# Splitting the operands of the third down-projection tile one round earlier, into two free weight slots

## The chip, the core and the metric

The kernel runs on one core of a Trainium2 chip. The metric is the device time of one execution in microseconds. A core has a matrix engine (PE, with its weight loads as PEld), a vector engine (DVE), an activation engine (ACT), a general engine (POOL), and SP, which here only issues DMAs. Each takes its instructions from a queue of its own, in order, and waits at the head of the queue until the semaphores that the instruction names have been raised.

## What is computed

The input x is 2 sequences of 1024 rows of 512 numbers. Four sublayers follow one another, each on a layer norm of its input and with a residual: a gated linear attention, a feed-forward block, a softmax attention, and the same feed-forward block again. The change is in the feed-forward block:

```python
def _L0_ffn_ref(x, wq_gate, s_gate, wq_up, s_up, wq_down, s_down):
    def _qlinear(x, wq, scale):
        W = (wq.astype(jnp.float32) - ZERO_POINT) * scale[:, None]
        return jnp.einsum('bsd,hd->bsh', x, W)
    gate = jax.nn.silu(_qlinear(x, wq_gate, s_gate))
    up = _qlinear(x, wq_up, s_up)
    return _qlinear(gate * up, wq_down, s_down)
...
x = x + _L0_attn_a_ref(_layernorm(x), ...)
x = x + _L0_ffn_ref(_layernorm(x), ...)
x = x + _L0_attn_b_ref(_layernorm(x), ...)
x = x + _L0_ffn_ref(_layernorm(x), ...)
```

The hidden width is 1408 = 11 x 128.

## The kernel before

**Halves.** The function `ffn` runs twice: with the name "f" (from x1 to x2) and "g" (from x3 to the output). The 2048 rows are 16 tiles of 128; each `ffn` takes them in two halves `pr` of 8 tiles, so there are four half-blocks: f pr 0, f pr 1, g pr 0 and g pr 1. In each, gate rounds come first and down projections after.

**Gate rounds.** Round `j` (of 11) computes 128 hidden columns for the 8 tiles with seven products P1 to P7 into four PSUM tiles X, Y, Z and V (`products`, L303). Between the products ACT copies X and Z (L728, L731) and DVE combines Y, Z and V (L729 and L732 to L734). `finish` of a round is issued one round later: it adds P2, P3 and P4, ACT applies silu (L702, L703), DVE multiplies gate by up (L705, L706, L709), and the result lies in three places: tiles 0 and 1 in `sg`, tiles 2 and 3 in `ha`, tiles 4 to 7 in `hb`. `finish` of round 10 stands after the loop.

**Splits.** PE multiplies rounded fp32 numbers, so an operand is given as a rounded high part and a remainder. `split` (L85, L86) does that: ACT casts to the high part, DVE (or POOL) subtracts it from the source. The down projection of tile `i` reads its operands, 11 x 128 columns high and as many low, from the tile `hs[i]`. The pool for `hs` has two buffers. Tiles 0 and 1 take them and are split round by round inside `finish`. Tile 2 can be split only when tile 0's last product has read its buffer, tile 3 when tile 1's has, and so on.

**Down projections.** For tile `i`, PE makes 22 products of 128x512: high and low part of each of 11 hidden blocks, by the weights `wd` (L760, L761). DVE scales the sum by `sd_b` (L762), POOL adds the residual `xr` that SP has loaded (L764, L753), and SP stores the tile (L768). Ahead of tile `i` the code splits tile `i`+1, in two pieces of 768 and 640 columns (6 and 5 blocks).

**Other work beside them.** While the tiles run, `late` steps are taken two at a time: in pr 0 those of `combine` for the second half (sums of layer-normed rows on DVE, L244, and splits of 1024 columns into operands named B11, T1, B22, T2, T3, B21 and T4). After f pr 0 the layer norms for the softmax attention (tiles named b0 to b7 here) can begin as soon as their rows of x2 are stored: SP loads `xin_b` (L106), DVE makes statistics (L108 to L112), POOL a power (L114), DVE the normed rows (L116) and a transpose (L187). `behind(done)` puts the `late` steps behind the latest split on the ACT and DVE queues.

**Slots.** A pool of 12 buffers of 128x2048 ("slots") holds gate weights (`wc`, up to three rounds ahead, loaded by L292), the operands made by `combine`, the transposed rows `xT`, and the weights of the attention (`wm`, `wvo`).

**What sets the order.** The program order gives priorities. When the kernel is built, a scheduler with its own idea of durations lays the instructions of every engine into a fixed queue, filling what it takes for gaps with instructions of lower priority, and gives out buffers as they come free in its plan. At run time nothing is reordered.

The loop ahead of the products, before the change:

```python
done = finish(*begun)
wcs = []
for i in range(2 * ST):
    if 1 <= i < 2 * ST - 1:
        n = i + 1
        for js in (slice(0, 6), slice(6, KH)):
            done = h_split(n, js, ha[:, n - 2, js] if n < ST else hb[:, n - ST, js], None)
```

Of the kernel before, what the change touches and what calls it, by code (L numbers as in the profile page):

```python
# [10 lines left out]
F32R = mybir.dt.float32r  # L11
# [5 lines left out]
P = 128  # L17
# [7 lines left out]
KH = HID // P  # L25
ST = 4
# [8 lines left out]
def hybrid_block_kernel(ctx: ExitStack, tc: tile.TileContext, a, out):  # L35
    nc = tc.nc
# [12 lines left out]
    def slot(name, dt=F32R):  # L49

        return wp.tile([P, 2048], dt, tag="slot", name=name)
# [31 lines left out]
    def split(hi, lo, src, eng=None):  # L83

        c = nc.scalar.copy(hi, src)  # L85
        return c.ins, (eng or nc.vector).tensor_tensor(lo, src, hi.bitcast(F32), ALU.subtract).ins  # L86
# [125 lines left out]
    def ln_steps(src, nm, st):  # L212

        return [lambda i=i: ln_norm(src, nm, st, i) for i in range(ST)] + [
            lambda b=b: ln_move(nm, st, b) for b in range(4)
        ]
# [78 lines left out]
    def products(ps, w, nm, pr, n, first):  # L295
        m, x = {
            "P1": (1, "B11"), "P2": (5, "B21"), "P3": (6, "B22"), "P4": (7, "T4"),
            "P5": (2, "T1"), "P6": (3, "T2"), "P7": (4, "T3"),
        }[n]
        o = XT[nm, pr, x]  # L300
        for k in range(2):
            for s in range(2):
                nc.tensor.matmul(  # L303
                    ps,
                    w[:, m, k * P : (k + 1) * P],
                    o[:, s, k, :],
                    start=first and k == 0 and s == 0,
                    stop=k == 1 and s == 1,
                    skip_group_check=n != "P6",
                )  # L310
# [358 lines left out]
    def ffn(src, dst, nm, wcs, after):  # L669


        with ExitStack() as fctx:
            fh = fctx.enter_context(tc.tile_pool(name=f"ffnh{nm}", bufs=1))
            f1 = fctx.enter_context(tc.tile_pool(name=f"ffn1{nm}", bufs=2))
            fw = fctx.enter_context(tc.tile_pool(name=f"ffnw{nm}", bufs=KH))
            fp = fctx.enter_context(tc.tile_pool(name=f"ffn{nm}", bufs=4))
            wd = []
            for pr in range(2):
                if pr == 0:
                    early = ln_steps(src, nm, 2) + ln_steps(src, nm, 3)  # L680
                    late = combine(nm, 1)
                else:
                    early, late = (list(x) for x in after)

                ha = fh.tile([P, 2, KH, P], F32, tag="ha", name=f"ha{nm}{pr}")
                hb = fh.tile([P, ST, KH, P], F32, tag="hb", name=f"hb{nm}{pr}")
                hs = {}

                def h_split(i, js, src, eng):
                    if i not in hs:  # L690
                        hs[i] = f1.tile([P, 2, KH, P], F32R, tag="hs", name=f"hs{nm}{pr}_{i}")
                    return split(hs[i][:, 0, js], hs[i][:, 1, js], src, eng)

                def finish(j, w, X, Z, V, up):

                    products(X, w, nm, pr, "P2", False)
                    products(Z, w, nm, pr, "P3", False)
                    products(V, w, nm, pr, "P4", False)
                    tiles = lambda x: x.rearrange("p (i c) -> p i c", c=P)
                    su = su_s[:, j : j + 1]  # L700
                    sg = fp.tile([P, 512], F32, tag="sg", name=f"sg{nm}{pr}_{j}")
                    nc.scalar.activation(sg, X, AF.Silu, scale=sg_s[:, j : j + 1])  # L702
                    nc.scalar.activation(hb[:, :, j], tiles(Z), AF.Silu, scale=sg_s[:, j : j + 1])  # L703
                    h01 = sg[:, 0:256]
                    nc.vector.scalar_tensor_tensor(h01, V[:, 0:256], su, h01, ALU.mult, ALU.mult)  # L705
                    nc.vector.scalar_tensor_tensor(  # L706
                        ha[:, :, j], tiles(V[:, 256:512]), su, tiles(sg[:, 256:512]), ALU.mult, ALU.mult
                    )
                    nc.vector.scalar_tensor_tensor(hb[:, :, j], tiles(up), su, hb[:, :, j], ALU.mult, ALU.mult)  # L709
                    for i in range(2):  # L710
                        done = h_split(
                            i,
                            j,
                            h01[:, i * P : (i + 1) * P],
                            None if j == KH - 1 or (nm == "f" and pr == 0) else nc.gpsimd,
                        )
                    return done

                begun = None
                for j in range(KH):  # L720
                    for n in range(len(wcs), min(j + 3, KH)):
                        wcs.append(stationary(n, f"{nm}{pr}", (xp, "xres") if nm == "f" and pr == 0 else None))
                    w = wcs[j]
                    X, Y, Z, V = (psum(f"p{n}{nm}{pr}_{j}") for n in "XYZV")
                    for ps, n in ((X, "P1"), (Y, "P6"), (Z, "P5"), (V, "P7")):
                        products(ps, w, nm, pr, n, True)
                    u2 = fp.tile([P, 512], F32, tag="sg", name=f"u2{nm}{pr}_{j}")
                    nc.scalar.copy(u2, X)  # L728
                    nc.vector.tensor_tensor(u2, Y, u2, ALU.add)  # L729
                    up = fp.tile([P, 512], F32, tag="sg", name=f"up{nm}{pr}_{j}")  # L730
                    nc.scalar.copy(up, Z)  # L731
                    nc.vector.tensor_tensor(Z, Z, u2, ALU.add)  # L732
                    nc.vector.tensor_tensor(V, V, u2, ALU.add)
                    nc.vector.tensor_tensor(up, V, up, ALU.add)  # L734
                    if begun:
                        finish(*begun)
                    begun = j, w, X, Z, V, up
                    for _ in range((1, 1, 1, 1, 2, 2, 1, 1, 1, 1, 2)[j] if early else 0):
                        early.pop(0)()
                    if pr == 0:  # L740
                        d = fw.tile([P, 512], F32R, tag="wd", name=f"wd{nm}{j}")
                        nc.sync.dma_start(out=d.bitcast(F32), in_=wd_d[j])
                        wd.append(d)
                done = finish(*begun)
                wcs = []
                for i in range(2 * ST):
                    t = pr * 2 * ST + i
                    if 1 <= i < 2 * ST - 1:
                        n = i + 1
                        for js in (slice(0, 6), slice(6, KH)):  # L750
                            done = h_split(n, js, ha[:, n - 2, js] if n < ST else hb[:, n - ST, js], None)
                    xr = xp.tile([P, D], F32, tag="xres", name=f"xr{nm}{t}")
                    nc.sync.dma_start(out=xr, in_=src[t])  # L753
                    o = fp.tile([P, 512], F32, tag="sg", name=f"o{nm}{t}")

                    last = nm == "g" and t == NT - 1
                    for ds in [slice(0, 256), slice(256, 512)] if last else [slice(0, 512)]:
                        ps = psum(f"po{nm}{t}_{ds.start}")[:, ds]
                        for j in range(KH):
                            nc.tensor.matmul(ps, hs[i][:, 0, j], wd[j][:, ds], start=j == 0, stop=False)  # L760
                            nc.tensor.matmul(ps, hs[i][:, 1, j], wd[j][:, ds], start=False, stop=j == KH - 1)  # L761
                        nc.vector.tensor_tensor(o[:, ds], ps, sd_b[:, ds], ALU.mult)  # L762
                        add = nc.vector if last else nc.gpsimd
                        add.tensor_tensor(xr[:, ds], o[:, ds], xr[:, ds], ALU.add)  # L764
                        if last:
                            nc.sync.dma_start(out=dst[t][:, ds], in_=xr[:, ds])
                    if not last:
                        nc.sync.dma_start(out=dst[t], in_=xr)  # L768
                    with behind(done):
                        for _ in range(2 if i > 0 else 0):  # L770
                            if early or late:
                                (early or late).pop(0)()
                    if pr == 0 and i == 4:
                        wcs = [stationary(n, f"{nm}1") for n in range(2)]

    ffn(
        x1,
        x2,
# [8 lines left out]
    with ExitStack() as bctx:  # L787
# [3 lines left out]
        for dst, d, n in ((wm, m_d, "wm"), (wvo, vo_d, "wvo")):  # L791
            two = [slot(f"{n}{m}") for m in range(2)]
# [228 lines left out]
```

## Time and profile before

| | us |
|---|---|
| three runs | 1000.64, 1002.87, 1003.65 |
| median | 1002.87 |
| the profiled execution | 1001.88 |
| span of its instructions | 1000.2 |
| PE busy in the span | 959.9 (96%) |
| PEld busy | 789.7 (79%) |
| DVE busy | 682.6 (68%) |
| ACT busy | 374.6 (37%) |
| POOL busy | 228.5 (23%) |

The profiled execution is 1.68 us longer than its span, which is what lies around the first and last instruction, and 0.99 us under the median. In the timelines below, times count from the start of the span. The four down-projection stages begin in full at about 341 (f pr 0), 457 (f pr 1), 846 (g pr 0) and 958 us (g pr 1). A line of a timeline has the start, the duration, the engine, the source line and operation, the tiles written and read with the buffer numbers left out, and in brackets the idle time ahead of it with what ended it.

### The profile page before, as it was taken

To read this page: it belongs to the slowest core of one execution; us is meant where nothing else is said; L and a number is where in the kernel's file an instruction comes from. 1 tells how busy PE (TensorE), PEld (TensorE's weight loads), DVE (VectorE), ACT (ScalarE), POOL (GpSimd) and SP (SyncE) were. 2 spreads that over 40 slices of the span, in tenths; PEclk is the share of its full clock that TensorE was granted. 3 is DMA by queue.
4 is the path that set the end of the run, shared out by engine and by line. 5 is a ranking of instruction groups with operands and counts; after the bars stand their busy time and mean duration, and the time that the engine had idled before them with its cause. 6 is when DMAs were issued, how large, how long until landed. Compare 5 with 4: busy or idle time off the path is not lost.

```text
span 1000.2 us, 13108 instructions
## 1 busy us (share of the span) xinstructions
PE 959.9 (96%) x4450; PEld 789.7 (79%) x4450; DVE 682.6 (68%) x1294; ACT 374.6 (37%) x719; POOL 228.5 (23%) x281
## 2 busy tenths in 40 slices
PE   8999999979898999999999999999988999999998
PEld 6788888867686777887888888888866888788877
DVE  6766858769876699786526556356586675976665
ACT  4653334232665433443222223222133443444421
POOL 4442323253644133212200000000000111321122
PEclk9999999989999999999999999999988999999999
DMA  8636463564698555752704766427768763464113
GB/s 265 204 102 169 126 168 129 153 165 157 234 357 234 143 205 203 185 144 74 262 22 94 167 152 163 101 63 153 168 157 288 250 158 66 151 222 163 38 52 96
DMA packets 250996, 160.08 MB, mean 160 GB/s; under 512 B 187760, under 2 KB 203440, under 8 KB 250928
## 3 DMA queue, kind: packets, MB, share of 16 engines
q1 hardware_dynamic: 250928, 159.23, 54.2%
q8 instruction: 35, 0.57, 0.2%
q14 instruction: 33, 0.27, 0.1%
HBM read 102.66 MB, written 41.84 MB: 144 GB/s over the span
## 4 chain that ended last, share of the span: by engine, by line
PE 52%; DMA 3%; DVE 3%; SPq 2%; ACT 1%; issue 0%; POOL 0%; ACTq 0%; POOLq 0%; DVEq 0%
PE pZg L303 4%; PE pVg L303 4%; PE pXg L303 4%; PE pog L761 4%; PE pog L760 4%; PE pob L96 2%; PE psc L96 2%; PE psc L97 2%; PE pob L97 2%; PE pob L98 2%; PE psc L98 2%; PE pYg L303 2%; PE pof L761 2%; PE pVf L303 2%; PE pof L760 2%; PE pZf L303 2%
## 5 line engine op out<-in xcount | busy, mean ns | idle before, releaser
L761 PE MATMUL pof<-wdf,hsf 128*128 128x512 f32 x176 | 68.4, 392 | 4.5 <-DVE hsf L86 4.5
L761 PE MATMUL pog<-wdg,hsg 128*128 128x512 f32 (+1 forms) x187 | 69.0, 378 | 3.0 <-DVE hsg L86 3.0
L760 PE MATMUL pog<-wdg,hsg 128*128 128x512 f32 (+1 forms) x187 | 69.1, 378 | 0.0
L760 PE MATMUL pof<-wdf,hsf 128*128 128x512 f32 x176 | 68.2, 391 | 0.0
L96 PE MATMUL pob<-vh,pth 128*128 128x512 f32 x128 | 51.8, 405 | 5.7 <-ACT pth L85 5.7
L96 PE MATMUL psc<-xh_b,qh 128*128 128x512 f32 x128 | 51.5, 402 | 0.0
L97 PE MATMUL psc<-xT_b,qh 128*128 128x512 f32 x128 | 51.4, 402 | 0.0
L98 PE MATMUL psc<-xh_b,ql 128*128 128x512 f32 x128 | 51.3, 400 | 0.0
L97 PE MATMUL pob<-vl,pth 128*128 128x512 f32 x128 | 51.2, 400 | 0.0
L303 PE MATMUL pXf<-B_f,wcf 128*128 128x512 f32 x176 | 47.8, 401 | 3.4 <-ACT u2f L728 2.3
L98 PE MATMUL pob<-vh,ptl 128*128 128x512 f32 x128 | 50.8, 398 | 0.0
L303 PE MATMUL pVf<-T_f,wcf 128*128 128x512 f32 x176 | 46.7, 392 | 1.4 <-DVE upf L734 0.7
L303 PE MATMUL pXg<-B_g,wcg 128*128 128x512 f32 x176 | 47.2, 389 | 0.0
L303 PE MATMUL pVg<-T_g,wcg 128*128 128x512 f32 x176 | 46.7, 389 | 0.0
L86 POOL TENSOR_TENSOR hsg<-sgg,hsg 128x128 fp32r<-128x128 f32 x40 | 17.6, 461 | 120.9 <-ACT hsg L85 94.9
L837 ACT ACTIVATE pe<-psc,nm 128x512 f32<-128x512 f32 x32 | 21.7, 683 | 62.7 <-DVE nm L832 62.7
L761 PEld LDWEIGHTS pof<-wdf,hsf 128*128 128x128 f32 x176 | 33.1, 188 | 12.7 <-DVE hsf L86 5.9
L761 PEld LDWEIGHTS pog<-wdg,hsg 128*128 128x128 f32 x187 | 35.1, 188 | 10.0 <-DVE hsg L86 3.6
L303 PEld LDWEIGHTS pXf<-B_f,wcf 128*128 128x128 f32 x176 | 33.0, 191 | 12.7 <-ACT u2f L728 3.9
L85 ACT CAST pth<-ptl 128x512 fp32r<-128x512 f32 x30 | 17.1, 618 | 68.0 <-DMA ptl<-p 57.5
L764 POOL TENSOR_TENSOR xrf<-of,xrf 128x512 f32<-128x512 f32 x16 | 25.0, 1563 | 76.6 <-DVE of L762 54.0
L114 POOL TENSOR_TENSOR rs_g<-ve_g,mhalf 128x1 f32<-128x1 f32 x16 | 10.5, 667 | 139.0 <-DVE ve_g L112 123.7
(286 smaller groups left out, 2642.9 us busy)
## 6 DMA issues: line engine op xcount, KB each, us to landing
wcg<-wc SPq DMA_DIRECT2D x22, 896.0 KB, 4.9
wc<-wcf SPq DMA_DIRECT2D x11, 896.0 KB, 4.4
wcf<-wc SPq DMA_DIRECT2D x11, 896.0 KB, 4.9
p<-py SPq DMA_DIRECT2D x15, 512.0 KB, 3.0
ptl<-p SPq DMA_DIRECT2D x60, 128.0 KB, 3.0
xin_a<-in_x SPq DMA_DIRECT2D x16, 256.0 KB, 4.4
xra<-in_x SPq DMA_DIRECT2D x16, 256.0 KB, 3.0
row<-cl SPq DMA_DIRECT2D x16, 256.0 KB, 4.2
```

What stands on the lines that cost most here:

```text
L85: c = nc.scalar.copy(hi, src)
L86: return c.ins, (eng or nc.vector).tensor_tensor(lo, src, hi.bitcast(F32), ALU.subtract).ins
L96: nc.tensor.matmul(ps, lhs_hi, rhs_hi, start=first, stop=False)
L97: nc.tensor.matmul(ps, lhs_hi, rhs_lo, start=False, stop=False)
L98: return nc.tensor.matmul(ps, lhs_lo, rhs_hi, start=False, stop=last).ins
L114: nc.gpsimd.tensor_tensor(rs, ve, mhalf, ALU.pow)
L303: nc.tensor.matmul(ps, w[:, m, k * P : (k + 1) * P], o[:, s, k, :], start=first and k == 0 and s == 0, stop=k == 1 and s == 1, skip_group_ ...
L760: nc.tensor.matmul(ps, hs[i][:, 0, j], wd[j][:, ds], start=j == 0, stop=False)
L761: nc.tensor.matmul(ps, hs[i][:, 1, j], wd[j][:, ds], start=False, stop=j == KH - 1)
L764: add.tensor_tensor(xr[:, ds], o[:, ds], xr[:, ds], ALU.add)
L837: nc.scalar.activation(pe[:, s * 512 : (s + 1) * 512], pS[s], AF.Exp, bias=nm, scale=SC, accum_out=rs[:, s : s + 1],).ins
```

## The change

Tile 2 no longer waits for tile 0's buffer. Its high and low parts get a slot each from the pool of 12. Ten of its eleven hidden blocks are split ahead of the last `finish` (one cast and one subtraction of 1280 columns), the eleventh after it. The loop then splits tile `i`+2 ahead of tile `i`, starting with tile 3 at i = 1. The pool of two `hs` buffers stays and now serves tiles 0, 1, 3, 4, 5, 6 and 7. The numbers of products, evictions, residual adds and transfers stay the same.

```diff
 def h_split(i, js, src, eng):
     if i not in hs:
-        hs[i] = f1.tile([P, 2, KH, P], F32R, tag="hs", name=f"hs{nm}{pr}_{i}")
-    return split(hs[i][:, 0, js], hs[i][:, 1, js], src, eng)
+        if i == 2:
+            two = [slot(f"hs{nm}{pr}_{i}{n}") for n in "hl"]
+            hs[i] = [x[:, 0 : KH * P].rearrange("p (j c) -> p j c", j=KH) for x in two]
+        else:
+            both = f1.tile([P, 2, KH, P], F32R, tag="hs", name=f"hs{nm}{pr}_{i}")
+            hs[i] = both[:, 0], both[:, 1]
+    hi, lo = hs[i]
+    return split(hi[:, js], lo[:, js], src, eng)
...
+h_split(2, slice(0, KH - 1), ha[:, 0, 0 : KH - 1], None)
 done = finish(*begun)
+h_split(2, KH - 1, ha[:, 0, KH - 1], None)
 wcs = []
 for i in range(2 * ST):
     t = pr * 2 * ST + i
-    if 1 <= i < 2 * ST - 1:
-        n = i + 1
+    if 1 <= i < 2 * ST - 2:
+        n = i + 2
         for js in (slice(0, 6), slice(6, KH)):
             done = h_split(n, js, ha[:, n - 2, js] if n < ST else hb[:, n - ST, js], None)
...
-            nc.tensor.matmul(ps, hs[i][:, 0, j], wd[j][:, ds], start=j == 0, stop=False)
-            nc.tensor.matmul(ps, hs[i][:, 1, j], wd[j][:, ds], start=False, stop=j == KH - 1)
+            nc.tensor.matmul(ps, hs[i][0][:, j], wd[j][:, ds], start=j == 0, stop=False)
+            nc.tensor.matmul(ps, hs[i][1][:, j], wd[j][:, ds], start=False, stop=j == KH - 1)
```

## The prediction, made before the changed kernel was run

> **What bounds the kernel now.** I read the page's busy shares first: PE is busy 96% of the span, so a change gains where PE waits, or not at all. The costliest groups come next, for the idle time ahead of the down projections:
>
> ```profile
> L761 PE MATMUL pof<-wdf,hsf 128*128 128x512 f32 x176 | 68.4, 392 | 4.5 <-DVE hsf L86 4.5
> L761 PE MATMUL pog<-wdg,hsg 128*128 128x512 f32 (+1 forms) x187 | 69.0, 378 | 3.0 <-DVE hsg L86 3.0
> ```
>
> The idle time ends with DVE's remainder of `hs`: 7.5 us in all. The PE timeline says where; these are the lines with idle time in the four down-projection stages:
>
> ```profile
> 349.68 0.50 PE L761 MATMUL pof<-wdf,hsf 128*128 128x512 f32 x1 [1.52 <-DVE hsf L86]
> ...
> 366.16 0.50 PE L761 MATMUL pof<-wdf,hsf 128*128 128x512 f32 x1 [1.23 <-DVE hsf L86]
> ...
> 390.60 1.20 PE L303 MATMUL pVf<-T_f,wcf 128*128 128x512 f32 x4 [0.65 <-DVE of L762]
> ...
> 464.71 0.50 PE L761 MATMUL pof<-wdf,hsf 128*128 128x512 f32 x1 [1.48 <-DVE hsf L86]
> ...
> 854.45 0.50 PE L761 MATMUL pog<-wdg,hsg 128*128 128x512 f32 x1 [1.49 <-DVE hsg L86]
> ...
> 966.17 0.50 PE L761 MATMUL pog<-wdg,hsg 128*128 128x512 f32 x1 [1.53 <-DVE hsg L86]
> ```
>
> Four gaps of 1.5 us are the first low part of tile 2, one in each stage. The others, with one of 0.23 at 371.68, lie in f pr 0 and where it runs into f pr 1. The timelines of ACT, DVE and POOL around 462 us show what tile 2 waits for:
>
> ```profile
> 461.84 2.82 ACT L85 CAST hsf<-haf 128x768 fp32r<-128x768 f32 x4 [4.88 <-PE pof L761]
> ...
> 461.79 0.69 DVE L762 TENSOR_TENSOR of<-pof,sd_b 128x512 f32<-128x512 f32 x1 [4.50 <-PE pof L761]
> 462.71 1.94 DVE L86 TENSOR_TENSOR hsf<-haf,hsf 128x768 fp32r<-128x768 f32 x1 [0.23 <-ACT hsf L85]
> ...
> 462.56 1.28 POOL L764 TENSOR_TENSOR xrf<-of,xrf 128x512 f32<-128x512 f32 x1 [9.64 <-DVE of L762]
> ```
>
> Tile 0's last product frees the buffer; then follow tile 0's eviction, the cast, and a subtraction that takes 1.94 us because POOL's add runs beside it (the same shape takes 0.94 at 358.41, with POOL idle). ACT had been idle 4.88 us and DVE 4.50 us just before.
>
> How close DVE is to being the bound: the table by stretches for the end of f pr 0, and DVE's waits from 340 to 400.
>
> ```profile
> 362.00:370.00 8.00, 6.77 (x30) 5.25 (x30) 8.00 (x11) 4.14 (x6) 3.96 (x3) 1.00 0.73 285
> 370.00:378.00 8.00, 7.78 (x35) 6.07 (x34) 8.00 (x10) 4.41 (x5) 3.19 (x2) 1.00 0.41 131
> ...
> DVE bn_b L108 <- DMA xin_b<-x: 2.1, 1, 2.1
> DVE xn_b L116 <- POOL rs_b L114: 1.7, 1, 1.7
> ```
>
> The columns are the stretch, its length, then busy time of PE, PEld, DVE, ACT and POOL. DVE (third) is busy all 8.00 us of both: in this stage DVE sets the pace, PE follows.
>
> **What the Trainium skill says.** "Perfetto Trace Analysis", Optimization Strategy: the same gap repeating on the engine that should be saturated can mean too few buffers for the next tile. The trace agrees: 1.48 to 1.53 us, four times, and the buffer of tile 0 ends each. "GPSIMD Engine Reference", Key points: GpSimd shares SBUF interfaces with VectorE and contends with vector instructions of two SBUF inputs; agrees, 1.94 against 0.94. "DMA: Bandwidth & Descriptors", Anatomy of one DMA: about 2 us of a transfer are fixed (given for GpSimd's path; these go by SP). The `xin_b` loads land in 2.9 to 6.2 us, median 4.8: the fixed part is there, other transfers add the rest. "TensorE: Matmul & The Clock Gate", What's actually happening: an idle window of about 3.4 us halves the clock. Agrees: after a PE gap of 3.43 us (ending at 734.94) the granted clock is 0.59 over the next 7 us.
>
> **The change, part by part.**
>
> *The gap of tile 2.* The high product before it starts at 462.74, the low one at 464.71; without a wait products start 0.23 apart, so the loss is 1.97 - 0.23 = 1.74. By the same subtraction the others are 1.76 (f pr 0), 1.75 (g pr 0), 1.79 (g pr 1): 7.04 together.
>
> *The early split.* A cast of 1280 columns: ACT rows of 768 and 1024 take 0.84 and 1.05, so about 1.26. The subtraction: 0.94 and 1.19, so about 1.44. In f pr 1 the cast runs from 452.2 (after round 9's casts) to 453.5 and the subtraction to 454.9; the next on either queue are the silu at 454.28 and the product at 455.01. Both fit. In f pr 0 round 10's hb product goes from 339.98 to about 340.2; it must be split when PE reaches block 10 of tile 0 at 345.9, and is at about 342.3. Cost nothing; without the 3.6 us of cover the 0.2 would show. The two slots were last read by round 8's weights and by the first product of round 10, long over. So tile 2 is ready whenever PE is.
>
> *What is late next.* Tile 3's split now stands where tile 2's did, ready some 2.8 to 3.8 us after tile 0 ends, while PE has the rest of tile 1 and 22 x 0.227 = 5.0 us of tile 2: over 2 us spare. From tile 5 on two buffers alternate as before: a split may start when tile i-2 ends and has the 5.0 us of tile i-1.
>
> *f pr 1, g pr 0, g pr 1.* In g pr 0 `combine` loads DVE too, and the changed queue has tile 3's eviction ahead of `combine`'s next sum, so DVE idles some 2.8 us there; but tile 4 is split a tile sooner. Adding up the queue, tile 5's first piece is done at 865.6 (needed 867.7), 6's at 871.7 (872.7), 7's at 877.1 (878.8), T4 at 888.0 (after 892): all in time. In f pr 1 and g pr 1 DVE idles anyway (23.37 of 35 us busy from 465 to 500). Gain kept: 1.74 + 1.75 + 1.79 = 5.28.
>
> *f pr 0 into f pr 1.* Here the scheduler has moved more. Layer norms b2 to b4 whole and the statistics of b5 and b6 are now ahead of, or among, the first combinations of f pr 1 (before: b0 to b3), T4's remainder is behind two of them, and on SP the weights of round 2 (`wc`, L292) stand behind tile 7's store. I added up DVE's queue from tile 0's eviction at 346.76, by start-to-start steps of the trace: 0.60 for a 512-column operation, 0.86 and 0.70 for a split's two pieces, 1.13 for 1024 columns, 0.58 statistics, 0.46 norm, 0.62 transpose, under 0.1 for small ones, 1.0 more where a POOL add falls on a two-input SBUF operation (six of them), 4.8 for a load of b0 and b1, 2.9 to 4.8 after. Each load is followed on SP by waits for DVE's norm and for stores, so b0 is not there until 356.2 (DVE free at 354.5) and b6 not until about 393. First pieces: tile 5 at 362.9, 6 at 368.5, 7 at 376.3; Z of round 0 at 391.8, of round 1 at 394.2. PE, without the gap, would want them at 362.9, 368.1, 374.8, 389.3 and 392.8. Its waits are 0.1, 0.45, 1.6, 2.6 and 1.5: 6.25 us. Before, the waits after tile 2 were 1.23 + 0.23 + 0.65 and about 0.2 of restart each, 2.7. The stage gives back 3.6 and has gained 1.76: **1.9 us slower**. Bounds: with loads at 2.9 the waits shrink to 3.8 less tile 2's, a gain of 0.6; with the loads at 6.2 it loses 1.4 more at b0 and b1 together, 1.8 at b5 and 1.9 at b6: 7.0.
>
> *Sum:* -5.28 + 1.9 = -3.4. Against the profiled execution's 1001.88: 998.5; its median lies 0.99 higher, so 999.5.
>
> **The rivals.**
>
> *All four gaps are gained* (-7.0, 995.9). For it: work and transfers are the same in number, and DVE has 1.6 us less in the crowded stretch. Against it: DVE is 8.00 of 8.00 busy, and the norms come sooner.
>
> *The f boundary eats the gain* (-1 to +1.7, about 1003). At 6.2 us per load it loses 7.0 and the sum is +1.7. Against it: half of the eight loads landed in 4.8 us or less.
>
> *Slower.* One mechanism at one place: the waits of DVE for `xin_b` at the head of f pr 1, with the first Z combinations queued behind, keep PE idle more than 3.4 us in one piece, and the clock halves. Price: 7.0 with the loads at 6.2, and a low clock as after the gap at 734.94 costs (1 - 0.59) x 7 = 2.9, so 9.9 - 5.28 = +4.6, 1007.5. It decides from a boundary loss of 5.28 + 3 = 8.3 on. For it: 2.6 us is already my longest single wait there. Against it: all loads must be at their slowest.
>
> *That the change doesn't do what it says* would need the slots to be taken late; their last readers speak against it.
>
> **How the numbers follow.** About 0.3%, 3.0 us, is what a measurement of this kernel can tell from no change. Likeliest case (three gaps kept, part given back): 0.55, at 999.5; all four kept 0.17; eaten 0.17; slower 0.11. Faster than 999.87: the second, and some 0.33 of the first, 0.50. Slower: the last and a little of the third, 0.13. The rest, 0.37, is within. Range: 996.0, just above the best case, to 1004.5, the loads at their slowest; what is left out is the slow case and a small tail below.
>
> **What would show it.** Right: no gap ahead of tile 2 at 347.7, 462.7, 851 and 963, and a 1280-column subtraction ahead of the last hb product; the tiles of f pr 1 and g gap-free; the gaps of f pr 0's end moved to tile 7 and to the Z products of rounds 0 and 1, with DVE waiting for `xin_b`. Wrong: a gap at tile 3, one at tile 0's block 10 (the early split then delayed `finish`), new gaps in g pr 0, or a boundary of f that is as dense as before.

## The result, and the profile after

| | before | after | ratio (95% interval) |
|---|---|---|---|
| median of 14 runs each, us | 1000.55 | 999.81 | 0.9989 (0.9976 to 1.0002) |
| a second series (35 and 12 runs) | 1001.33 | 1000.51 | 0.9990 (0.9971 to 1.0009) |
| the profiled execution, us | 1001.88 | 1000.46 | |
| span, us | 1000.2 | 998.4 | |

The change moves the time by less than can be told apart from nothing. That is not because nothing happened. The costliest groups on the page after, with busy time, mean duration, and idle time ahead of the group:

```profile
L769 PE MATMUL pof<-wdf,hsf 128*128 128x512 f32 x154 | 59.8, 392 | 1.2 <-DVE hsf L86 1.2
...
L769 PE MATMUL pog<-wdg,hsg 128*128 128x512 f32 (+1 forms) x165 | 60.5, 375 | 0.0
```

The idle time ahead of the low products was 4.5 us in f and 3.0 in g; it is now 1.2 and 0.0. (The counts fall by 22 because tile 2 now reads tiles of another name and is listed apart.) The PE timeline shows the lines with idle time from f pr 0's down projections to the q projection:

```profile
366.69 0.50 PE L769 MATMUL pof<-wdf,hsf 128*128 128x512 f32 x1 [0.27 <-DVE hsf L86]
...
374.85 0.50 PE L769 MATMUL pof<-wdf,hsf 128*128 128x512 f32 x1 [0.16 <-DVE hsf L86]
...
379.11 0.50 PE L769 MATMUL pof<-wdf,hsf 128*128 128x512 f32 x1 [0.74 <-DVE hsf L86]
...
394.98 3.86 PE L303 MATMUL pZf<-B_f,wcf 128*128 128x512 f32 x8 [2.65 <-DVE pZf L738]
...
398.64 1.91 PE L303 MATMUL pXf<-B_f,wcf 128*128 128x512 f32 x4
```

Tile 2 waits nowhere. One new gap, of 2.65 us, stands ahead of the Z products of round 0 of f pr 1. Look also at the durations behind it. These eight products take 3.86 us; before, they took 1.98 us and had no wait ahead of them:

```profile
393.48 1.98 PE L303 MATMUL pZf<-B_f,wcf 128*128 128x512 f32 x8
```

The table by stretches of 3.4 us (length, then busy PE, PEld, DVE, ACT, POOL, then the granted clock, DMA share and GB/s) says why:

```profile
387.70:391.10 3.40, 3.40 (x17) 2.82 (x16) 3.40 (x7) 0.00 (x0) 2.12 (x2) 1.00 0.27 92
391.10:394.50 3.40, 1.24 (x6) 0.70 (x4) 3.40 (x6) 1.63 (x2) 0.92 (x2) 0.99 0.77 224
394.50:397.90 3.40, 2.92 (x7) 2.11 (x8) 3.40 (x6) 1.38 (x2) 0.45 (x1) 0.50 1.01 413
397.90:401.30 3.40, 3.40 (x10) 2.66 (x9) 2.98 (x7) 1.27 (x2) 0.34 (x1) 0.50 1.01 385
401.30:404.70 3.40, 3.40 (x17) 2.81 (x16) 2.61 (x5) 1.23 (x2) 0.21 (x1) 1.00 0.25 98
```

The clock is 0.50 for two stretches, 6.8 us. PE reads as fully busy in the second of them, with 10 products where 17 fit: busy share doesn't show a halved clock, the count and the clock column do.

To compare kernels I cut the execution at points that all of them have, and took starts from the timelines:

| stage, us | before | after | difference |
|---|---|---|---|
| **F**: f pr 0's first down-projection product to the first X product of round 8, f pr 1 | 95.97 | 98.89 | +2.92 |
| the rest of f pr 1's rounds | 19.98 | 19.95 | -0.03 |
| f pr 1's down projections, to the q projection | 38.91 | 37.13 | -1.78 |
| g pr 0's down projections, to round 8 of g pr 1 | 93.54 | 91.78 | -1.76 |
| g pr 1's down projections, to the last product | 43.86 | 42.05 | -1.81 |

Three gaps of tile 2 are gained, 5.35 us, and F gives 2.92 of them back. What remains of the difference between the two executions lies where the code is the same: after starts f 2.83 us later, and the stretch from its q projection to g pr 0's down projections is 2.43 us shorter, in traces with half-clock stretches at different places. The stages of the table sum to -2.46 us, and to -3.88 with the F of a second trace (experiment 5), while the medians moved by only -0.74 and -0.82. Of this difference 0.36 us lies outside the span (2.08 us in the changed kernel's runs, 1.72 in the runs of the kernel before in the second series); where the rest goes is not shown.

**FF** below is F and the two rows after it, from f pr 0's first down-projection product to the q projection: 154.86 before, 155.97 after. Its 651 products come 0.227 us apart where nothing waits, so it can't be shorter than 147.8 (my expectations say 147.6). Subtracting 0.227 from each start-to-start distance gives what every wait and every half-clock product cost. In after, the waits at tiles 5, 6 and 7 cost 0.54, 0.43 and 1.02 us, the one at Z 2.81, and the 15 half-clock products behind it **3.09**. (My expectations have 3.55 for them; that took in small delays elsewhere.)

The same subtraction before gives 1.87 us at tile 2, 1.50 and 0.50 at tiles 5 and 6, and 0.92 ahead of the V products at 390.60: 4.79 in F, against 4.80 for the four waits in after. So in F the change didn't shorten PE's waiting. It moved most of it into one place, and the clock did the rest. Nor is round 0's Z ready later than before, counted from the start of F (334.94 before, 338.18 after). Before, the addition that completes it is

```profile
391.67 0.69 DVE L732 TENSOR_TENSOR pZf<-pZf,u2f 128x512 f32<-128x512 f32 x1
```

and starts 56.73 us into F; in after (394.25) it is 56.07. PE is there earlier, because it no longer waits at tile 2, and because its own queue changed too: before, eight X and Y products (1.8 us) stand between those V products and these Z products; in after, the Z products come first.

### The profile page after: what moved, and what is told of

Its sections match the earlier page's. It is cut to its first block, busy times and chain, and to the rows that moved or that the text cites. A ratio compares the mean times of both kernels' runs of the same rounds, so it can differ in the third digit from the quotient of the medians.

```text
span 998.4 us, 13096 instructions
## 1 busy us (share of the span) xinstructions
PE 962.7 (96%) x4450; PEld 791.4 (79%) x4450; DVE 685.4 (69%) x1294; ACT 374.7 (38%) x719; POOL 227.2 (23%) x281
## 4 chain that ended last, share of the span: by engine, by line
PE 55%; DMA 7%; DVE 4%; SPq 3%; issue 2%; POOL 1%; ACT 1%; DVEq 0%; ACTq 0%; POOLq 0%
PE pog L769 4%; PE pog L768 4%; PE pXg L303 4%; PE pVg L303 4%; PE pZg L303 4%; PE pZf L303 2%; PE pof L769 2%; PE pof L768 2%; SPq L196 2%; PE pob L96 2%; PE psc L96 2%; PE psc L97 2%; PE psc L98 2%; PE pVf L303 2%; PE pob L98 2%
## 5 line engine op out<-in xcount | busy, mean ns | idle before, releaser
L769 PE MATMUL pof<-wdf,hsf 128*128 128x512 f32 x154 | 59.8, 392 | 1.2 <-DVE hsf L86 1.2
L768 PE MATMUL pog<-wdg,hsg 128*128 128x512 f32 (+1 forms) x165 | 60.6, 375 | 0.0
L769 PE MATMUL pog<-wdg,hsg 128*128 128x512 f32 (+1 forms) x165 | 60.5, 375 | 0.0
L768 PE MATMUL pof<-wdf,hsf 128*128 128x512 f32 x154 | 59.5, 390 | 0.0
L114 POOL TENSOR_TENSOR rs_b<-ve_b,mhalf 128x1 f32<-128x1 f32 x16 | 10.7, 667 | 130.0 <-DVE ve_b L112 130.0
L303 PEld LDWEIGHTS pVf<-T_f,wcf 128*128 128x128 f32 x176 | 32.9, 188 | 8.1 <-DVE upf L740 1.4
```

The lines of the kernel that those rows point to most:

```text
L114: nc.gpsimd.tensor_tensor(rs, ve, mhalf, ALU.pow)
L303: nc.tensor.matmul(ps, w[:, m, k * P : (k + 1) * P], o[:, s, k, :], start=first and k == 0 and s == 0, stop=k == 1 and s == 1, skip_group_ ...
L768: nc.tensor.matmul(ps, hs[i][0][:, j], wd[j][:, ds], start=j == 0, stop=False)
L769: nc.tensor.matmul(ps, hs[i][1][:, j], wd[j][:, ds], start=False, stop=j == KH - 1)
```

## The experiments

My theory after the comparison: the slots take away tile 2's gap everywhere; in F, DVE now has more of the attention's layer norms ahead of round 0's combination of Z; that makes the 2.65 us gap; and the gap costs 2.8 us itself and some 3 more by the clock. The rivals: the half-clock stretch is chance; or the norms don't matter and DVE is simply full.

Every ratio below is to the kernel before, run beside the experiment on the same chip; stage times are of one profiled execution each.

(My expectations call the Z products behind the gap those of round 1. By the order of DVE's additions the first four are round 0's, the next four round 1's.)

### 1. The change without f pr 0

```diff
-if i == 2:
+if i == 2 and not (nm == "f" and pr == 0):
...
-if 1 <= i < 2 * ST - 2:
-    n = i + 2
+if 1 <= i < 2 * ST - ahead:   # ahead is 1 in f pr 0, else 2
+    n = i + ahead
```

(Shortened: where `ahead` is 1, tile 2's early split is left out as well.)

> The change is made in three of the four half-blocks (f pr 1, g pr 0, g pr 1); f pr 0 stays as in the kernel before. Stage F is the time from f pr 0's first down-projection product to the first X product of round 8 in f pr 1: 95.97 us before, 98.89 after. My theory (the change saves tile 2's gap in three half-blocks and loses 2.9 us in stage F, because a PE gap of 2.65 us ahead of round 1's Z products there is followed by 6.8 us at half clock): stage F is back at 96.0, no half-clock window starts between 390 and 400 us, and the three other stages keep -1.78, -1.76 and -1.81; the total is about 5.3 us below the kernel before, a ratio of 0.995. Rival (that half-clock window has nothing to do with the change, it falls where it likes): the window is found in stage F in this kernel too, or stage F differs from 96.0 by more than 0.5.

Ratio 0.9964 (0.9948 to 0.9979). F is 95.63, with the gaps of before (1.52, 1.12, 0.24, 0.68) and no half-clock stretch; the three other stages are 37.13, 91.78 and 42.05. FF is 152.72. The loss is tied to the change in f pr 0: leaving it out there saves more than making it.

### 2. The change in f pr 0 alone

The condition of experiment 1 is reversed, in the same lines.

> The change is made in f pr 0 alone. My theory: stage F (f pr 0's first down-projection product to the first X product of round 8 in f pr 1) shows what the whole change showed there: no gap at tile 2, gaps of about 0.3, 0.2 and 0.7 us at tiles 5 to 7, one of 2.65 us ahead of round 1's Z products, then 6.8 us at half clock, 98.9 in all against 95.97; the other down-projection stages keep their gap of 1.5 us; the total is 2.9 above before, a ratio of 1.003. Rival (the window is chance): the gaps are there, the half-clock window isn't, and stage F is about 95.8, a total like before's.

Ratio 1.0016 (1.0000 to 1.0032), where I expected 1.003. F is 98.79. The PE timeline at the end of F's down projections:

```profile
389.05 1.20 PE L303 MATMUL pZf<-B_f,wcf 128*128 128x512 f32 x4 [2.62 <-DVE pZf L738]
...
390.83 2.08 PE L303 MATMUL pZf<-B_f,wcf 128*128 128x512 f32 x4 [0.59 <-DVE pZf L738]
```

The gap is here again, and the second four products already run at half clock. The half-clock stretch lasts 3.4 us from 390.5 on. The other stages keep their gap (38.94, 93.53, 43.86). Experiments 1 and 2 together: the change acts by half-block, and F is where it hurts.

### 3. The gap filled with matmuls

```diff
-products(ps, w, nm, pr, n, True)
+for _ in range(4 if nm == "f" and pr == 1 and j == 1 and n == "P7" else 1):
+    products(ps, w, nm, pr, n, True)
```

> The whole change, and in f pr 1 the product P7 of round 1 is computed four times in place of once (12 matmuls more, the same values into the same tile), just ahead of the Z products that wait for DVE. It fills the 2.65 us gap with 12 x 0.23 = 2.8 us of matmuls. If the lost time is the halved clock (my theory): no half-clock window starts between 385 and 405 us and stage F is about 98.89 - 3.0 + 0.1 = 96.0, although PE has 2.8 us more to do; the total is 3 below after. Rival (the wait itself is the loss, the clock window is chance or costs nothing there): stage F stays at 98.9 or grows, by up to 2.8.

Ratio 0.9960 (0.9940 to 0.9979). There is no half-clock stretch between 250 and 730 us. The stretch that held the gap, with the columns as above:

```profile
389.50:392.90 3.40, 3.40 (x16) 2.59 (x15) 3.40 (x7) 1.64 (x2) 0.60 (x2) 1.00 0.90 279
```

FF is 154.53, which is 1.44 us less than after although PE has 12 more products, 2.72 us, to do. F is 97.45 and not the 96.0 that I expected: with the clock up, the wait for round 1's Z, which the half-clock products had covered, shows (0.59 us), and tile 5 waited 0.92 in place of 0.27. Products put into idle time should cost nothing; that they shorten FF fits only the clock that stayed up. Against the second trace of after (experiment 5, FF 154.56, half the time at low clock) FF is merely the same, so the clock column and experiment 4 carry as much of this as the time.

### 4. The gap made shorter

As experiment 3, with P7 twice in place of four times.

> The whole change, and product P7 of round 1 in f pr 1 computed twice (4 matmuls more, the same values): the 2.65 us gap ahead of the Z products shrinks by 4 x 0.227 = 0.9 to about 1.75 us. If the clock follows how much of a stretch of some 3.4 us PE idles (my theory; in the six traces so far it halved after stretches with PE busy for 44% or less, and not after one with 54%): no half-clock window at 390 to 400, stage FF about 155.97 - 3.55 = 152.4 (the added products take the place of idle time). Rival (any wait of over a microsecond or so there does it): the window is there, FF about 156.

One execution. The table by stretches, laid on this trace's own grid:

```profile
386.70:390.10 3.40, 3.40 (x17) 2.81 (x16) 3.40 (x5) 0.56 (x1) 1.89 (x2) 1.00 0.51 116
390.10:393.50 3.40, 1.66 (x8) 0.95 (x6) 3.40 (x8) 1.36 (x3) 0.55 (x1) 1.00 0.96 335
393.50:396.90 3.40, 2.80 (x13) 2.12 (x12) 3.40 (x7) 1.74 (x3) 0.00 (x0) 1.00 1.05 416
```

The gap is 1.74 us, PE is busy for 1.66 of the 3.40 us, and the clock stays at 1.00. FF is 153.82, against 155.97 and, in the second trace of after, 154.56. I had expected 152.4; round 1's wait of 0.60 and its restart (0.87 together) are again what I left out, and the 3.55 that I took off is 3.09.

### 5. The changed kernel again

> The changed kernel itself once more, to see whether the half-clock stretch at the boundary of f comes again, since its place in the trace hangs on stretches of 3.4 us whose start shifts from run to run. My theory: PE gaps of 2.6 to 2.7 us ahead of round 1's Z products again, and 3.4 or 6.8 us at half clock right behind it; stage FF 154 to 156. Rival (the window was chance): the gap without the window, FF about 152.4.

The gap is 2.65 us once more, and one stretch at half clock follows it, not two:

```profile
391.00:394.40 3.40, 1.14 (x6) 0.60 (x4) 3.40 (x6) 1.63 (x2) 0.91 (x2) 0.99 0.74 212
394.40:397.80 3.40, 3.00 (x7) 2.19 (x8) 3.40 (x6) 1.38 (x2) 0.36 (x1) 0.50 1.01 424
397.80:401.20 3.40, 3.40 (x17) 2.79 (x16) 3.40 (x8) 1.39 (x3) 0.42 (x1) 1.00 1.02 385
```

F is 97.47 and FF 154.56; the half-clock products cost 1.53 us. With experiment 2, the gap of 2.6 us was followed by a half-clock stretch in three traces of three, and the shortened or filled one in none of two. So few traces don't make it certain for every run (see the last section). How long the clock stays low differs from run to run, so F's loss was 2.92 in one trace and 1.50 in the other.

### 6. The norms held back

```diff
-nc.vector.tensor_tensor(V, V, u2, ALU.add)
+mixed = nc.vector.tensor_tensor(V, V, u2, ALU.add).ins
...
-for _ in range((1, 1, 1, 1, 2, 2, 1, 1, 1, 1, 2)[j] if early else 0):
-    early.pop(0)()
+with behind((mixed,) if nm == "f" and pr == 1 else ()):
+    for _ in range((1, 1, 1, 1, 2, 2, 1, 1, 1, 1, 2)[j] if early else 0):
+        early.pop(0)()
```

> The whole change, and in f pr 1 each gate round's steps of the layer norms for the softmax attention are held behind that round's last addition to V, so DVE has none of them ahead of the combinations of round 0 and 1. My theory (the norms and their loads, moved ahead of these combinations, are what makes round 1's Z late): no PE gap over 0.7 us at rounds 0 and 1, no half-clock window between 385 and 405 us, stage F about 94.2 to 94.8 (95.97 less tile 2's 1.76, give or take the small waits), and the total about 7 us below the kernel before, ratio 0.993. Rival (DVE's plain work of splits and sums sets the pace there, with or without norms): a gap of 1 to 2 us stays at round 0 or 1, stage F is 96 or more, ratio 0.995 or above. A second way to lose: the held norms come late for the attention, and the stage after f pr 1 grows by what they are late.

Ratio 0.9948 (0.9928 to 0.9968), FF 151.28, F 94.98; I had expected 0.993 and an F of at most 94.8. From 335 to 425 us PE has no gap at all. Between the start of F and round 0's combination of Z, DVE has none of the norms' statistics (6 in after, 4 before) and is busy for 38.9 us (47.3 in after, 44.7 before); that combination starts 50.42 us into F in place of 56.07. So the norms set when Z is ready, and the rival that they don't matter falls. That the two statistics added by the change made the gap is not shown by this, since Z was no earlier before the change (56.73). But 2.5 us of the gain turned into a new wait, which I had not listed. PE at round 7:

```profile
427.37 1.17 PE L303 MATMUL pXf<-B_f,wcf 128*128 128x512 f32 x4 [2.47 <-DMA wcf<-wc]
```

and SP's queue at that time (the second figure runs from a group's first issue to the end of its last):

```profile
398.18 0.86 SPq L292 DMA_DIRECT2D wcf<-wc  x2
406.31 6.66 SPq L106 DMA_DIRECT2D xin_b<-x  x2
413.90 6.14 SPq L196 DMA_DIRECT2D xT_b<-y_b  x8
420.14 0.57 SPq L292 DMA_DIRECT2D wcf<-wc  x1
```

The held norms free their buffers later, so the loads of `xin_b` block SP for longer (from 385 to 430 SP waits 14.6 us for `xn_b`, 3.1 in after), and the weights of round 7 stand behind them and behind eight transposing transfers. They are issued at 420.14, and PE gets them at 427. Counted from the start of F this is only 0.8 us later than in after (80.9 and 80.0). PE is what moved: in after it begins round 7 93.45 us into F, here it is ready at about 85.4.

### 7. The norms held, and begun two rounds later

```diff
-for _ in range((1, 1, 1, 1, 2, 2, 1, 1, 1, 1, 2)[j] if early else 0):
+for _ in range(((0, 0, 1, 1, 1, 1, 2, 2, 2, 2, 2) if nm == "f" and pr == 1
+                else (1, 1, 1, 1, 2, 2, 1, 1, 1, 1, 2))[j] if early else 0):
```

(with the edit of experiment 6 and the whole change; the long line is broken here)

> The whole change, the norms of f pr 1 held behind each round's last addition to V, and none of their 14 steps in rounds 0 and 1 (0, 0, 1, 1, 1, 1, 2, 2, 2, 2, 2 in the 11 rounds in place of 1, 1, 1, 1, 2, 2, 1, 1, 1, 1, 2). On SP the gate weights of round 7 then stand ahead of three of the four norm loads and of the transposing stores that made them late in the run with the norms held alone (issued at 420.14, landed after 427, PE waits 2.47 us). My theory: that wait goes, no gap over 0.5 us is left in stage FF, which is 151.28 - 2.5 = 148.8 (651 products at 0.227 would take 147.6); total ratio to before 0.992 or lower. Rival (SP and the transfers are full there; the load that is late is only another): a gap of 1 to 2.5 us for weights comes back at round 8 or 9, or the norms are late for the q projection and its first product waits as long: FF 150 to 151.5.

Ratio 0.9916 (0.9896 to 0.9936): median 992.54 against 1001.31 for the kernel before on the same chip. FF is 148.14, 0.4 us over the 147.8 in which nothing would ever wait. The table by stretches (columns as above):

```profile
340.00:370.00 30.00, 30.00 (x133) 24.73 (x132) 19.66 (x24) 12.02 (x18) 7.16 (x5) 1.00 0.38 113
370.00:400.00 30.00, 30.00 (x134) 24.84 (x133) 27.29 (x33) 12.13 (x19) 5.36 (x5) 1.00 0.73 253
400.00:430.00 30.00, 30.00 (x135) 24.82 (x134) 26.32 (x54) 14.25 (x30) 6.55 (x14) 1.00 0.42 134
430.00:460.00 30.00, 30.00 (x133) 24.70 (x132) 24.25 (x51) 12.49 (x26) 6.25 (x12) 1.00 0.50 117
```

PE is busy throughout, with 133 to 135 products in each 30 us (125 in the same part before, from 366 to 396). DVE is still 27.29 of 30 us busy from 370 to 400: it had room for its work, only not in the order of after. The rival that DVE is simply full falls.

### 8. and 9. The norms held, without the slots

The edits of 6 and of 7, made to the kernel before.

> The kernel before, with the layer norms of f pr 1 held behind each round's last addition to V, as in the run with the whole change and the norms held. Stage FF is the time from f pr 0's first down-projection product to the first product of the q projection after f pr 1: 154.86 us before, 155.97 after, 152.72 with the change left out of f pr 0, 151.28 with the whole change and the norms held (there all PE gaps at tiles and at rounds 0 and 1 are gone, and one of 2.47 for a weight load is new). If the two edits act apart (my theory: holding the norms is worth about what the gaps at tiles 5, 6 and round 0 cost, the slots what tile 2 costs): the gaps of 1.5 us at tile 2 stay in all four half-blocks, the gaps of 1.23, 0.23 and 0.65 at the boundary shrink to under 0.5 together, and stage FF is 154.86 - 2.5 = 152.4, with 2.5 more if a weight load is late here too. If holding the norms alone does nothing (rival: only the whole change's norms were too early): FF stays at 154.9.

> The kernel before with the norms of f pr 1 held and begun in round 2, as in the run of the whole change with the norms held later. It completes a table of two edits (slots and two ahead: no, yes; norms held later: no, yes). Stage FF (f pr 0's first down-projection product to the q projection): before 154.86, whole change alone 155.97, both 148.14. If the norms were the whole trouble of the boundary and tile 2's gap stands apart (my theory): the gaps after tile 2 go (1.23, 0.23 and 0.65 with a restart of about 0.2 to 0.3 each, 2.9 in all), tile 2's stay, FF is about 151.9 and the total some 3 us below before, ratio 0.997; the change is then worth 3.6 in FF and 3.6 in g on top of it. Rival (without the slots DVE stays late there): gaps of over 1 us stay at tiles 4 to 7, FF 153 or more.

Ratios 0.9998 (0.9981 to 1.0015) and 0.9982 (0.9968 to 0.9996), FF 154.30 and 154.02: less gain than I expected of both (152.4 and 151.9). The gaps after tile 2 in F do go, as expected. But in f pr 1 tile 2 now waits twice: at its first high product, for the cast, and at its first low one as before. In both traces a half-clock stretch follows. The PE timeline of experiment 9, and the stretches around it:

```profile
459.13 0.50 PE L761 MATMUL pof<-wdf,hsf 128*128 128x512 f32 x1 [0.75 <-ACT hsf L85]
461.11 0.50 PE L762 MATMUL pof<-wdf,hsf 128*128 128x512 f32 x1 [1.48 <-DVE hsf L86]
```

```profile
458.20:461.60 3.40, 1.17 (x4) 0.63 (x4) 3.40 (x4) 3.36 (x6) 2.64 (x2) 1.00 0.60 133
461.60:465.00 3.40, 3.40 (x10) 2.61 (x9) 3.40 (x4) 0.50 (x1) 0.60 (x1) 0.50 0.68 147
```

Two waits, neither over 1.5 us, fell into one stretch, and the clock halved for 3.4 us. So the two edits don't simply add in FF: norms held later alone -0.84, the whole change alone +1.11 (-0.30 in the second trace), both -6.72. Each leaves a wait that the other takes away.

### 10. The slots alone, later tiles split one ahead

```diff
-if 1 <= i < 2 * ST - 2:
-    n = i + 2
+if 2 <= i < 2 * ST - 1:
+    n = i + 1
```

> One part of the change alone: tile 2 in two slots, split in the last gate round, but the later tiles split one ahead as before. My theory (the gap of tile 2 goes with the slots; two ahead only moves work): the stages of f pr 1 (from its first down-projection product to the q projection), of g pr 0 (to the first X product of round 8 in g pr 1) and of g pr 1 (to the last product) are 37.1, 91.8 and 42.1 as with the whole change, against 38.9, 93.5 and 43.9 before; in f pr 0 no gap at tile 2. At the boundary of f the queue order is another again, so I expect gaps there of 2 to 5 us in all: stage FF 151.5 to 156. Rival (two ahead is needed): a gap of over 0.5 us at tile 3 or 4 in f pr 1 or g, where before there was none, and these stages 0.5 or more longer than with the whole change.

Ratio 0.9934 (0.9913 to 0.9955). The stages of f pr 1 and g are 37.13, 91.78 and 42.05, as with the whole change: the slots do all of that. In F:

```profile
372.50 0.50 PE L769 MATMUL pof<-wdf,hsf 128*128 128x512 f32 x1 [1.69 <-DVE hsf L86]
...
390.76 1.20 PE L303 MATMUL pVf<-T_f,wcf 128*128 128x512 f32 x4 [0.93 <-DVE of L770]
```

Two gaps are left, with time between them, no half-clock stretch, and FF 151.24, just under my range. Splitting two ahead gains nothing in these traces. In F it costs 3 to 5 us: the scheduler laid the queues out differently behind it. DVE has 5 statistics ahead of round 0's Z, 6 in after, and the combination starts 53.93 us into F, 56.07 in after. On PE, eight X products stand between V's and Z's, none in after. Which single move of the queues does it was not separated further.

## Why the prediction was right, and where it was wrong

| step | predicted | measured |
|---|---|---|
| cast and subtraction of 1280 columns | 1.26, 1.44 | 1.25, 1.49 |
| tile 2 in f pr 1, g pr 0, g pr 1 | -1.74, -1.75, -1.79 | -1.78, -1.76, -1.81 |
| waits at tiles 5, 6, 7 of f pr 0 | 0.1, 0.45, 1.6 | 0.27, 0.16, 0.74 |
| waits at Z of rounds 0, 1 | 2.6, 1.5 | 2.65, 0 (0.59 and 0.60 at full clock) |
| half clock in F | not in the sum | 3.09; 1.53 in the second trace |
| F as a whole | +1.9 | +2.92; +1.50 |

The predicted 999.5 stands beside 999.81, but part of that is luck of the starting point. The prediction took 3.4 us off a level that rests on the median of three runs, 1002.87. Over 14 runs the kernel before has 1000.55, so the measured change is -0.74 us (-2.4 to +0.2) and not -3.4. The forecast ratio, 0.9966, lies below the interval. "Faster", the likeliest outcome at 0.50, did not come; "within", at 0.37, did.

**What held:** the early split is hidden. ACT and DVE have it ahead of the last hb product, and PE doesn't wait behind it:

```profile
340.58 1.25 ACT L85 CAST hsf_2h<-haf 128x1280 fp32r<-128x1280 f32 x1
```

```profile
341.86 1.49 DVE L86 TENSOR_TENSOR hsf_2l<-haf,hsf_2h 128x1280 fp32r<-128x1280 f32 x1 [1.59 <-ACT hsf_2h L85]
343.27 0.75 DVE L715 SCALAR_TENSOR_TENSOR hbf<-upf,cols,hbf 128x512 f32<-128x512 f32 x1
```

Tile 3 had its time to spare, and g pr 0, where DVE is loaded too, has no gap, as the sum of its queue said. The gap of 2.6 us at round 0's Z was found to 0.05 us by adding up DVE's queue, closer than the working deserves: its later waits missed by up to 0.9 us, at tile 6 it is the second piece that is late and not the first, and the times that it lists give waits of 0.0, 0.4, 1.5, 2.5 and 1.4, or 5.8 in all, not 6.25. Here is that queue in after, the stretch in which PE waits (392.3 to 394.98):

```profile
389.04 0.69 DVE L108 BATCH_NORM_STATS2 bn_b<-xin_b 128x6 f32<-128x512 f32 x1
389.64 0.67 DVE L770 TENSOR_TENSOR of<-pof,sd_b 128x512 f32<-128x512 f32 x1
390.23 0.53 DVE L116 TENSOR_SCALAR xn_b<-xin_b,mv_b,rs_b 128x512 f32<-128x512 f32 x1
390.69 2.31 DVE L244 TENSOR_TENSOR xT_f<-xT_f,xT_f 128x1024 f32<-128x1024 f32 x1
392.92 0.17 DVE L110 BATCH_NORM_AGGREGATE mv_b<-bn_b 128x2 f32<-128x6 f32 x1
393.01 1.25 DVE L735 TENSOR_TENSOR u2f<-pYf,u2f 128x512 f32<-128x512 f32 x2
394.19 0.14 DVE L112 TENSOR_SCALAR ve_b<-mv_b 128x1 f32<-128x1 f32 x1
394.25 0.68 DVE L738 TENSOR_TENSOR pZf<-pZf,u2f 128x512 f32<-128x512 f32 x1
```

DVE is never idle in it. Norm steps stand between the pieces that PE wants, and one sum takes 2.31 us beside a POOL add (1.18 to 1.22 for the same shape with POOL idle). It needn't be DVE that gives way: before, the sum at 383.55 took 1.21 us beside a POOL add that took 2.28.

**What failed.** First, the later waits at tile 7 and round 1 were put too high: I summed 6.25 us of waits, and they were 3.82 on the timeline, 4.80 with their restarts. I had put six POOL collisions and loads of up to 4.8 us one after another into one queue; DVE waited for `xin_b` only twice, 1.9 us in all, about as before (2.1). Second, the step "keep PE idle more than 3.4 us in one piece, and the clock halves" was wrong. I kept the clock out of the likeliest case because my longest single wait was 2.6. The runs show it halve after a single gap of 2.62 to 2.65 us, and after two of 0.75 and 1.48 close together. That term was put at 0 and measured 3.09 and 1.53. The two errors had opposite signs, 1.4 and 1.5 to 3.1 us, and most of them cancelled. The mechanism of the slow rival was at work, without a gap of 3.4 us and at a smaller price than the 9.9 that it was given.

The trace before could have told me. I looked at one gap of 3.43 us in it. Of its five half-clock stretches between 10 and 985 us, four follow stretches without a gap that long. The first is this one; PE's wait, then the stretch that holds it and the next:

```profile
207.71 1.55 PE L548 MATMUL pd<-sWv,kw 128*128 128x128 f32 x8 [2.62 <-POOL kw L530]
```

```profile
204.90:208.30 3.40, 0.78 (x7) 0.59 (x6) 1.78 (x8) 2.24 (x4) 2.28 (x4) 1.00 0.66 219
208.30:211.70 3.40, 3.40 (x19) 3.40 (x18) 3.40 (x7) 0.00 (x0) 1.14 (x3) 0.50 0.78 268
```

Of the "wrong if" signs, none came: no gap at tile 3, none at tile 0's block 10, none in g pr 0, and PE's waits after tile 2 in F, 2.9 us before, are 4.8.

## What to carry to other kernels

A buffer that comes free too late is cheaply replaced by one that is idle at that moment: 1.8 us in each place where nothing else was tight. Where another engine is nearly full, ask what its queue will look like after the edit: the scheduler moves other work too, and in f pr 0 what splitting two ahead brought with it cost 3 to 5 us, more than the gap that was removed. Then put the two together: with the slots and the norms held later, the kernel runs 0.8% faster than before, while the change as it stands and the held norms alone each gave 0.2% at most. Trying less of a change is cheap too: the slots with the later tiles split one ahead gave 0.7% by themselves, and these runs can't tell that from the 0.8% (0.9934 and 0.9916, with overlapping intervals).

## What the runs showed of the hardware that I had not expected

**The clock looks at stretches, not at gaps.** In each of the twelve traces all half-clock stretches begin on one grid of 3.413 us, whose start differs from trace to trace. The Trainium skill ("TensorE: Matmul & The Clock Gate", What's actually happening) states a free-running window of 3413 ns, which these traces agree with, and that the clock falls after an idle window. Here a half-idle one is enough. I estimated PE's share of each stretch from the starts of its matmuls (each counts until the next start, or 0.46 us at most), for the stretches between 10 and 985 us that were at full clock and not wholly busy:

| PE's share of the stretch | clock halved next | clock stayed |
|---|---|---|
| under 0.48 | 52 | 0 |
| 0.48 to 0.55 | 6 | 11 |
| 0.55 to 0.65 | 2 | 25 |
| 0.65 to 0.88 | 0 | 157 |

With the profile's own busy times for the share, the clock halved after 58 of 61, 2 of 14, 0 of 30 and 0 of 169: the edge is again near one half, and it is not sharp with either estimate.

So in the two traces of after the gap of 2.65 us (share 0.37 to 0.40 in the stretch that holds most of it) cost 5.9 and 4.3 us with the slow products behind it, about twice its length. A gap of 1.5 us alone that fell into one stretch left the share at 0.54 to 0.59 and cost only itself. Where a gap falls on the grid matters as much as its length: one of 3.15 us near 250 was followed by half clock in eleven traces, but not in that of experiment 3, where it lay across two stretches (PE busy for 1.95 and 1.69 of 3.40 us); the 2.47 us of experiment 6 lay across two as well (1.80 and 2.54), and the clock stayed. The half-clock time between 10 and 985 us was 34.1 us in one trace of after and 27.3 in the other, so a part of the differences between runs of one kernel may be a few such stretches more or less; that is not shown further.
